# A two-layer graph network on one core: one-column bias products as steps of their own, the last norm in smaller steps, and a new order of all steps

## The chip, the core and the metric

The kernel runs on one core of one Trainium2 chip. The time is device microseconds of one execution, median of the runs shown. The engines are TensorE (PE, with its weight loads PEld), VectorE (DVE), ScalarE (ACT), GpSimd (POOL) and SyncE (SP), which here issues the DMAs.

## The reference

Input are 128 graphs of 128 nodes with 256 features, `x`, and their adjacency `adj` of 0 and 1, all in fp32. Two layers follow one another:

```
layer 0:  q, k = x@Wq+bq, x@Wk+bk          (8 heads of 32)
          attn = softmax(q k^T / sqrt(32))
          out  = sum over r of (attn * (adj == r)) @ (x@Wv[r]+bv[r])
          x    = LN(x + out@Wo+bo; g1, beta1)
          x    = LN(x + gelu(x@W1+b1)@W2+b2; g2, beta2)      (256 -> 1024 -> 256)
layer 1:  twice (W1,a1), (W2,a2):  Wh = h@W; e = leaky_relu(Wh1 + Wh2^T, 0.2)
          att = softmax over axis 1 of where(adj > 0, e, -9e15);  h = att@Wh
          x    = LN(x + h; g_ln1, b_ln1)
          x    = LN(x + relu(x@w_ff1+b_ff1)@w_ff2+b_ff2; g_ln2, b_ln2)
```

The kernel adds the second bias of a feed-forward part to the input of that part ahead of time, so the first bias has to be reduced by W1 applied to it: b1 - W1^T b2 in layer 0, b_ff1 - w_ff1^T b_ff2 in layer 1. These two corrections are the one-column products of this change.

## The kernel before

The 16384 nodes are worked on in 32 groups of 512 (four graphs each). What one group needs is cut into Python generators, and each `next` of one is a **step**: a few instructions, often one product or a piece of the chain behind it. `in_order` (L1141 on) walks through three strings, `FRONT`, `STEADY` and `TAIL`, and does one step for each token. A token `a:1*3` is three steps of generator `a` of the group one behind the base. `FRONT` runs once for groups 0 and 1 with all weight loads and set-up, `STEADY` runs for g = 1 to 29, `TAIL` runs from g = 30 to the end. All of it stands in a manual schedule, so the order of the tokens is the order of every engine's queue: PE, ACT, DVE, POOL, and SP with its DMAs. There is no other planner.

The tokens that are spoken of here:

- `in`, `rest`, `L...`: loads of xT, of adj and x, and of weights. All go through SP's queue.
- `q`: projections to q, k and v (pq, pv at L715 and L728; from group 2 on as Winograd forms pqqa, pqqb, pvqa, pvqb at L785). `a`: scores ps (L855), exp (ACT, L862), mask pm (DVE, L871), pav (L925), denominators pden (L913), the output product pwo (L965). `d`: sums over heads for the denominators, with a DMA (es<-e) on SP.
- `n0` to `n3`: layer norm: bn_stats (L407), variance + eps and power (L425 DVE, L426 POOL), two passes for each graph (L441 DVE: first with mean and gain, then with root and offset), then planes of 16 bits (L461 ACT) and a DMA transpose (L464). `t`: what comes back is copied (L489 ACT) and summed for the Winograd forms (yS, L498 to L502, DVE).
- `f`, `fc` and `k`, `kc`: the two feed-forward parts, their products (ph and seeded, L521; po and seeded, L530) and the chains behind them (activation hT, L545 ACT; sums at L588 to L663, mostly DVE). The products have few PSUM banks, so each waits for the chain that empties its bank.
- `l`: the attention of layer 1: pw (L1042), edges (L1013 ACT, gs at L1023 and L1031 DVE), py (L1055), pg (L1068).
- `b1`, `c1`: the bias corrections by `without` (L338), two steps each: sixteen one-column products into one PSUM tile `pbias`, then one subtraction of 128x8 on DVE. For b1 the column `temp` is a slice cut from the loaded b2; such slices share a buffer with the first hT tile of group 0.
- `w1`, `w2`, `u1`, `u2`, `wqk`, `wv`: sums of weight blocks (L262 DVE) for the Winograd forms. `output_bias`: the correction of bo (pb, L1117).
- `z`: the last norm of the last group. `out`: a store of a group's result. `checks`: minima and maxima for the flag.

PSUM tiles from `mm_tile` turn in two buffers of one tag ("s"). The same two serve ps, pqqa and pvqa alternately, pw, py, pg, pwo, pden of the second half, and pbias.

At the end, the last group's norm is done in two pairs of graphs. After `TAIL` the program compares the collected `c_out` with itself (`same`, `good`), does the passes of pair 0 and stores it, and then makes a flag from `good` with a product `pflag`; the flag decides whether a general version has to run over again.

Of the kernel before, what the change touches and what calls it, by code (L numbers as in the profile page):

```python
# [25 lines left out]
P = 128  # L26
G = 4
# [96 lines left out]
in:0 Lqk*2 q:0 Lqk L1 Lqk q:0*2 Lh1 Lgat Lv q:0 L2 Lv q:0 L4 Lv Lv_ Lg1 q:0*2 rest:0 Lv q:0 a:0  # L124
L1 Lv_ a:0*2 d:0 a:0*3 Lv_ d:0 q:0*2 L2 d:0*2 Lgat a:0 L1 Lg2 d:0*2 L1 in:1 d:0 a:0 q:0 d:0 a:0
q:0 a:0*6 wqk a:0*3 L2 a:0 L2 a:0 q:0*2 q:1 d:0*2 L1 d:0 a:0 rest:0 gw rest:1 d:0 a:0 L1 q:1 Lgat
w2 d:0*2 L3 Lo d:0 Lg1 q:1 a:0 d:0 q:0 L3 q:0 a:0 bo:0 q:1*3 w1 q:1 Lg1 q:1 L4 a:0 w2 a:0 a:1 w2
a:1*2 a:0*2 a:1 a:0 a:1 d:1 L3 bo:0 a:0 a:1*2 Lg1 a:0*2 d:1 a:0*2 rest:2 q:1 d:1 a:0 d:1 a:0 n0:0
q:1 n0:0 q:1 n0:0*2 q:1 b1 d:1*2 n0:0 a:1 d:1 w1 output_bias d:1 Lgat n0:0 a:1 Lh1 n0:0 t0:0*2 w1
bo:0 q:1 a:1 b1 a:1 L3 output_bias q:1 t0:0 a:1 f:0 a:1*3 w1 w2 a:1 d:1*2 a:1 t0:0 gw a:1 t0:0  # L130
Lh2 t0:0 d:1 fc:0 a:1 q:1 Lh1 a:1*2 f:0 fc:0 d:1 fc:0 a:1 f:0 d:1*3 f:0 fc:0 rest:1 f:0 q:1 a:1
f:0 gw d:1 a:1*2 f:0 fc:0*2 a:1*3 Lh1 f:0 fc:0*2 bo:1 L4 fc:0 wqk f:0 u1 fc:0 f:0 fc:0 a:1 in:2
fc:0 a:1 f:0 wqk a:1 fc:0 a:1 fc:0 f:0 fc:0 bo:1 a:1 L3 f:0 gw f:0*3 fc:0 a:1*2 q:2 fc:0*3 a:1
f:0 n0:1 L3 fc:0*4 L4 n0:1 f:0 fc:0 q:2 n0:1*2 fc:0 bo:1 f:0 n0:1 f:0 fc:0 Lg2 f:0 fc:0*2 q:2*2
t0:1 f:0 n0:1 fc:0 f:0 n0:1 f:0 q:2 fc:0 f:1 u2 fc:0*2 q:2 fc:1 t0:1 n1:0*2 gw n1:0*2 t0:1 q:2
t0:1 n1:0 q:2 t0:1*2 c1 n1:0 fc:1 n1:0 q:2 wv t1:0*2 q:2 u1 f:1 gelu t1:0 l:0 fc:1 t1:0 u1 u2
l:0*3 c1 q:2 wv f:1 q:2 l:0*2 wqk l:0 f:1 l:0 q:2 l:0 f:1 fc:1*2 f:1 fc:1 q:2 fc:1 f:1 q:2 f:1
fc:1*2 u2 exp q:2 f:1 l:0 wv fc:1*2 l:0*3 q:2*2 l:0*2 a:2 f:1 q:2 l:0 a:2 l:0 a:2 l:0*2 a:2*2
fc:1 l:0*6 f:1 a:2 l:0 wv l:0*2 d:2 fc:1*2 l:0 f:1 fc:1 u2 a:2 fc:1 f:1 fc:1 f:1 q:2 u1 fc:1 f:1
fc:1 f:1 l:0 fc:1 f:1 l:0*2 q:2*2 fc:1 d:2 f:1 l:0 fc:1 l:0 q:2 l:0 q:2 f:1 l:0 q:2 d:2 l:0 d:2  # L140
l:0*3 Lh2 d:2 a:2 l:0*2 fc:1 l:0*3 fc:1 l:0 fc:1 n2:0 q:2 n2:0*2 q:2 n2:0 q:2 fc:1 f:1 n2:0 fc:1
d:2 f:1 q:2
"""
STEADY = """
fc:0 q:1 d:1 q:1 fc:0 f:0 d:1 n2:-1*2 t2:-1*2 q:1 f:0 a:1 fc:0 a:1 f:0 fc:0 t2:-1 a:1*2 t2:-1
k:-1 t2:-1 a:1 fc:0 a:1 kc:-1 t2:-1 d:1 a:1 k:-1 a:1 k:-1 a:1 kc:-1 d:1 rest:1 n1:0 kc:-1 a:1
n1:0 d:1*2 a:1*2 k:-1*2 a:1 k:-1 a:1 k:-1 kc:-1 d:1 kc:-1 d:1 a:1 d:1 k:-1 in:2 d:1 k:-1*2 n1:0
a:1 kc:-1*2 a:1 n1:0*2 kc:-1*2 a:1 bo:1 kc:-1 a:1 kc:-1 a:1 k:-1 kc:-1 a:1*2 n1:0*2 a:1 kc:-1
t1:0*2 a:1 kc:-1 t1:0 a:1 k:-1 l:0 kc:-1 bo:1 a:1 l:0*2 kc:-1 t1:0 kc:-1 a:1 l:0 a:1 n0:1 k:-1*3
l:0*2 q:2 n0:1 l:0 kc:-1 q:2 k:-1 l:0 kc:-1 bo:1 k:-1 l:0 n0:1 kc:-1 k:-1 kc:-1*3 q:2*2 n0:1*3  # L150
kc:-1*2 n0:1 l:0*3 k:-1 t0:1 k:-1 t0:1 k:-1 kc:-1 k:-1 kc:-1*3 k:-1 kc:-1 l:0 k:-1 t0:1 f:1 t0:1
l:0 kc:-1 q:2 t0:1 fc:1 l:0 t0:1 f:1 l:0*2 f:1*3 l:0*2 fc:1*2 q:2 l:0 f:1 kc:-1 q:2 l:0 q:2 f:1
l:0*3 fc:1 l:0 rest:2 f:1 l:0 fc:1 l:0 n3:-1 f:1 l:0*2 fc:1*3 f:1 fc:1 n3:-1 fc:1 n3:-1 fc:1*2
q:2 f:1 fc:1 q:2*2 fc:1 q:2 f:1*2 fc:1 f:1 fc:1 q:2 f:1 fc:1 q:2 f:1 fc:1 gelu q:2*2 fc:1 q:2
l:0*3 fc:1 f:1 l:0 q:2 a:2 l:0 f:1 fc:1 l:0 fc:1 a:2 l:0 q:2 l:0*2 a:2 l:0 exp l:0 a:2*2 q:2 l:0
a:2 f:1 q:2 d:2 a:2 l:0 q:2 l:0*2 fc:1 d:2 q:2 l:0 d:2 fc:1 d:2 q:2*2 d:2 a:2 l:0 fc:1 n2:0 q:2
n2:0*2 q:2 out:-1 n2:0 q:2 fc:1 f:1 n2:0 q:2 d:2 f:1 fc:1
"""
TAIL = """
n2:-1 fc:0 d:1 n2:-1 q:1 fc:0 q:1 f:0 q:1 d:1 t2:-1 a:1 fc:0 t2:-1*2 f:0 a:1 f:0 fc:0 a:1 fc:0  # L160
n1:0 t2:-1 rest:1 t2:-1 n1:0 a:1*4 d:1 a:1 n1:0 k:-1 a:1 t2:-1 kc:-1 n1:0*2 k:-1 kc:-1 k:-1 bo:1
k:-1 d:1*3 n1:0 a:1 kc:-1 n1:0 k:-1 d:1 t1:0*2 k:-1 d:1 k:-1 a:1 kc:-1 d:1 kc:-1 k:-1 a:1*2 bo:1
k:-1 d:1 kc:-1 k:-1 kc:-1*2 a:1 t1:0 l:0*2 a:1 l:0 a:1*3 l:0 t1:0 bo:1 kc:-1*4 l:0 k:-1*2 a:1 l:0
a:1*2 l:0 kc:-1 l:0*2 kc:-1 a:1*3 kc:-1*2 a:1*2 k:-1*2 kc:-1 a:1 k:-1 a:1 n0:1 kc:-1 k:-1 kc:-1*4
l:0 n0:1 k:-1 l:0 k:-1 kc:-1 l:0*2 n0:1*2 k:-1 l:0*2 kc:-1*2 k:-1 n0:1*2 kc:-1 l:0 n0:1 l:0*2
k:-1 t0:1 l:0 kc:-1 l:0 kc:-1 t0:1 k:-1 l:0*2 t0:1 l:0 kc:-1 l:0 kc:-1 t0:1 l:0 t0:1 l:0*2 kc:-1
l:0 f:1 l:0 fc:1 t0:1 l:0*3 fc:1 k:-1 f:1 l:0 fc:1 f:1*2 l:0 fc:1 l:0*3 f:1*2 l:0 fc:1*2 l:0*2
f:1 fc:1*2 f:1 kc:-1 fc:1 f:1 l:0 fc:1*3 f:1*2 k:-1 fc:1 f:1 l:0 fc:1 f:1 fc:1 n3:-1 fc:1*2 f:1*2
fc:1 l:0 f:1 fc:1 l:0 fc:1 l:0*2 f:1 fc:1 n2:0 f:1 fc:1 n2:0 fc:1 n2:0 fc:1 n2:0 gelu f:1*2
fc:1*2 n2:0*2 n3:-1 n2:0 fc:1*2 t2:0 fc:1 t2:0 f:1*3 exp t2:0 f:1 fc:1*3 k:0 t2:0 n1:1 t2:0 kc:0  # L170
n1:1*2 k:0 n1:1 k:0 n1:1*2 t2:0 k:0 n1:1 k:0 kc:0 k:0 kc:0 t1:1*3 k:0 kc:0 l:1*3 t1:1 l:1 kc:0*2
l:1*3 k:0 kc:0 l:1*2 k:0 kc:0*3 l:1*2 kc:0 l:1*3 kc:0 l:1 k:0 l:1 k:0 l:1 kc:0 k:0 l:1*2 kc:0 k:0
kc:0 l:1*2 n3:-1 l:1*7 kc:0*2 l:1*4 k:0 l:1*2 k:0 l:1*3 kc:0 l:1 kc:0 k:0*2 l:1*2 kc:0 l:1 kc:0*2
l:1 kc:0 l:1*4 kc:0 n2:1 kc:0 k:0 n2:1*4 k:0 kc:0 k:0 n2:1 kc:0 n2:1 t2:1 kc:0 k:0 t2:1 k:0 kc:0
t2:1 kc:0*2 k:0 k:1 t2:1*3 kc:1 k:1 k:0 kc:1*2 k:1*2 kc:1 k:1 kc:0 kc:1 k:1 kc:1 k:1 kc:1 k:1
kc:1*2 out:-1 kc:1 k:1*2 kc:1*2 k:1 kc:1 k:1 n3:0 kc:1 n3:0 k:1*3 kc:1*2 k:1*2 checks kc:1*6 k:1
kc:1 k:1 kc:1*2 n3:0 k:1*2 kc:1 k:1 kc:1*4 k:1 out:0 k:1 z:1 kc:1*2 z:1*2
# [11 lines left out]
def fast_pass(ctx, tc, a, out):  # L189
# [148 lines left out]
    def without(b, w, col):  # L338

        pb = mm_tile("pbias")  # L340
        for f in range(NF):
            h, m = divmod(f, NF // 2)
            for c in range(NCH):
                nc.tensor.matmul(
                    pb[:, f : f + 1], w[:, PLAIN[c][h], 0, m * P : (m + 1) * P],
                    col[:, c : c + 1], start=(c == 0), stop=(c == NCH - 1),
                )
        yield
        nc.vector.tensor_sub(b, b, pb[:, :NF])
        yield 1  # L350
# [61 lines left out]
    def added(S, i, p, po):  # L412
# [1114 lines left out]
```

## Time and profile before

| | us |
|---|---|
| median of 3 runs | 2650.34 (2647.93 to 2650.73) |
| the profiled execution | 2649.95 |
| its span, first to last instruction | 2648.2 |
| mean granted clock of TensorE | 0.994 |

Four stretches of 40 us of the first 160, one of the steady part and two of the tail, as busy microseconds of each engine:

| us | PE | PEld | DVE | ACT | granted clock |
|---|---|---|---|---|---|
| 0 to 40 | 35.08 | 20.11 | 16.88 | 16.43 | 0.96 |
| 40 to 80 | 34.13 | 28.42 | 29.34 | 21.82 | 0.90 |
| 80 to 120 | 40.00 | 35.86 | 32.05 | 19.47 | 0.88 |
| 120 to 160 | 34.93 | 28.90 | 22.71 | 27.13 | 0.91 |
| 2560 to 2600 | 35.64 | 29.90 | 29.72 | 27.44 | 1.00 |
| 2600 to 2640 | 36.37 | 33.22 | 31.36 | 15.16 | 1.00 |

PE's records overlap: a record of a product lasts longer than the time after which the next one starts. So a busy share near 100% doesn't say that PE ran at its peak, and the starts of successive products tell more than their lengths. In the timeline the columns are start, length, engine, line, operation, output and inputs by name, shapes and count, and in brackets an idle time before it with what released it. One product of the program shows as two records (fp32), so a product of two instructions of 256 columns is "x4". The groups of the steady part follow one another about every 80 us; the second pg product of a group starts at 235.0 in the first of them, and the following ones on average 80.4 us apart up to 2405.9.

### The profile page before, as it was taken

The page shows a single profiled execution, that of the slowest core. Times are in us where ns is not written, and L with a number is a line of the kernel's source. Part 1 is how long each engine was busy: PE and PEld are TensorE (multiplying, and loading weights), DVE is VectorE, ACT ScalarE, POOL GpSimd, SP SyncE. Part 2 cuts the span into 40 slices and gives each one's busy share as a digit, 9 for nine tenths or more (in the row PEclk, how much of TensorE's full clock was granted, in tenths as well). Part 3 has the DMA queues.
Part 4 walks back from the last instruction along what each step waited for, and adds up shares of the span by engine and source line. Part 5 has one row for each costly group of instructions (what it writes and reads, how often), then busy time and mean ns, then how long its engine had stood idle before and what let it go on. Part 6 is the DMA issues. An engine that isn't in the chain of part 4 may idle for free.

```text
span 2648.2 us, 54505 instructions
## 1 busy us (share of the span) xinstructions
PE 2603.5 (98%) x20842; PEld 2309.2 (87%) x20842; DVE 2246.1 (85%) x5907; ACT 1859.7 (70%) x3839; POOL 132.8 (5%) x137
## 2 busy tenths in 40 slices
PE   9999999999999999999999999999999999999998
PEld 6788988889888889888889888889888898888887
DVE  5688888888888888888888888888888888898876
ACT  4567676777776776776776776777767767767764
POOL 0000000000000000000000000000000000000000
PEclk9899999999999999999999999999999999999999
DMA  6223223322223322223232323222233223232311
GB/s 179 57 55 73 49 64 65 74 61 55 61 58 73 74 64 48 66 61 73 61 71 51 67 62 73 61 66 53 55 73 73 64 45 69 61 73 61 69 29 34
DMA packets 317372, 170.61 MB, mean 64 GB/s; under 512 B 222768, under 2 KB 295600, under 8 KB 317104
## 3 DMA queue, kind: packets, MB, share of 16 engines
q1 hardware_dynamic: 316000, 166.66, 28.0%
q8 instruction: 166, 2.72, 0.4%
q14 instruction: 102, 0.84, 0.1%
q10 hardware_dynamic: 1104, 0.40, 0.1%
HBM read 66.20 MB, written 16.90 MB: 31 GB/s over the span
## 4 chain that ended last, share of the span: by engine, by line
PE 74%; DVE 14%; ACT 8%; issue 2%; DMA 2%; SPq 0%; POOL 0%; DVEq 0%; ACTq 0%; POOLq 0%
PE po L530 15%; PE ph L521 12%; PE seeded L521 10%; PE seeded L530 9%; PE pw L1042 4%; PE pwo L965 4%; PE pqqa L785 4%; PE pqqb L785 3%; PE pav L925 3%; DVE x L441 2%; ACT pm L896 2%; PE py L1055 2%; DVE st L407 2%; PE pvqa L785 2%; ACT e L862 2%
## 5 line engine op out<-in xcount | busy, mean ns | idle before, releaser
L461 ACT COPY planes<-x 128x512 uint16<-128x512 uint16 x384 | 223.5, 615 | 197.8 <-DVE x L441 197.0
L489 ACT COPY yT<-pT 128x512 uint16<-128x512 uint16 x384 | 272.0, 764 | 114.0 <-DMA pT<-planes 113.7
L426 POOL TENSOR_TENSOR rs<-rs,mhalf 128x4 f32<-128x4 f32 x129 | 130.7, 1013 | 2444.2 <-DVE rs L425 1749.2
L862 ACT ACTIVATE e<-ps 128x512 f32<-128x512 f32 x256 | 136.2, 589 | 98.4 <-PE ps L855 65.0
L521 PE MATMUL ph<-yT,w_L_gnn_w_ff 128*128 128x256 f32 x768 | 198.3, 387 | 6.5 <-ACT hT L545 6.2
L521 PE MATMUL seeded<-yS,w_L_gnn_w_ff 128*128 128x256 f32 x768 | 199.9, 383 | 2.9 <-DVE yS L501 1.8
L521 PE MATMUL seeded<-yS,w_L_gnn_W 128*128 128x256 f32 x768 | 201.9, 386 | 0.0
L521 PE MATMUL ph<-yT,w_L_gnn_W 128*128 128x256 f32 x768 | 197.3, 379 | 0.0
L407 DVE BATCH_NORM_STATS2 st<-x 128x6 f32<-128x256 f32 x512 | 191.2, 415 | 3.5
L530 PE MATMUL po<-w_L_gnn_W,hT 128*128 128x128 f32 x1536 | 187.1, 275 | 0.0
L530 PE MATMUL po<-w_L_gnn_w_ff,hT 128*128 128x128 f32 x1536 | 187.0, 275 | 0.0
L530 PEld LDWEIGHTS po<-w_L_gnn_W,hT 128*128 128x128 f32 x1536 | 184.0, 192 | 3.2
L530 PEld LDWEIGHTS po<-w_L_gnn_w_ff,hT 128*128 128x128 f32 x1536 | 181.7, 192 | 1.7
L871 DVE TENSOR_TENSOR pm<-e,adj 128x512 f32<-128x512 f32 x256 | 172.2, 683 | 2.9 <-ACT e L862 0.7
L521 PEld LDWEIGHTS ph<-yT,w_L_gnn_w_ff 128*128 128x128 f32 x768 | 140.6, 190 | 38.9 <-ACT hT L545 18.5
L521 PEld LDWEIGHTS seeded<-yS,w_L_gnn_w_ff 128*128 128x128 f32 x768 | 141.8, 190 | 31.0 <-ACT seeded L617 6.4
L521 PEld LDWEIGHTS seeded<-yS,w_L_gnn_W 128*128 128x128 f32 x768 | 143.3, 191 | 28.0 <-ACT seeded L644 6.2
L521 PEld LDWEIGHTS ph<-yT,w_L_gnn_W 128*128 128x128 f32 x768 | 143.5, 190 | 18.4
L896 ACT COPY pm<-e 64x512 f32<-64x512 f32 x256 | 157.8, 616 | 1.6
L545 ACT ACTIVATE hT<-hT,c_L_gnn_b 128x256 f32<-128x256 f32 x256 | 112.7, 500 | 48.9 <-DVE hT L629 29.7
L545 ACT ACTIVATE hT<-hT,c_L_gnn_b_ff 128x256 f32<-128x256 f32 x256 | 115.7, 501 | 26.1 <-DVE hT L629 22.9
L1042 PE MATMUL pw<-wu,yT 128*128 128x260 f32 x512 | 130.6, 387 | 2.7 <-ACT yT L489 2.6
(195 smaller groups left out, 6288.1 us busy)
## 6 DMA issues: line engine op xcount, KB each, us to landing
es<-e SPq DMA_DIRECT2D x256, 128.0 KB, 2.4
xT<-in_xT_dram SPq DMA_DIRECT2D x32, 512.0 KB, 4.9
x<-in_x_dram SPq DMA_DIRECT2D x32, 512.0 KB, 4.2
out_dram<-x SPq DMA_DIRECT2D x31, 512.0 KB, 3.3
spread<-hbm SPq DMA_DIRECT2D x61, 256.0 KB, 3.9
adj<-in_adjT_dram SPq DMA_DIRECT2D x32, 256.0 KB, 3.1
pT<-planes SPq DMA_TRANSPOSE x192, 3.1
w_L_gnn_W<-in_L_gnn_W_dram SPq DMA_DIRECT2D x8, 256.0 KB, 4.8
```

What stands on the lines that cost most here:

```text
L407: nc.vector.bn_stats(st[:, b % 2, :], S["x"][:, b, :])
L426: nc.gpsimd.tensor_tensor(rs[:, bs], rs[:, bs], k.mhalf[:, bs], op=ALU.pow)
L461: nc.scalar.copy(planes[:, :, b], words)
L489: nc.scalar.copy(o.rearrange("p (b t h) -> p h b t", b=2, h=2), pT[:, :, :, c, :])
L521: nc.tensor.matmul(bank[:, s * TH : (s + 1) * TH], wa[:, form, 0, f * P : (f + 1) * P], m, start=start and s == 0, stop=True, skip_group_c ...
L530: nc.tensor.matmul(bank[:, s * P : (s + 1) * P], m[:, f, s * P : (s + 1) * P], wb_[:, form, f, :], start=start and s + f == 0, stop=True, ...
L545: nc.scalar.activation(o[:, s], o[:, s] if src is None else src[:, s * TH : (s + 1) * TH], func, bias=ba[:, f : f + 1],)
L785: nc.tensor.matmul(bank[:, s * TH : (s + 1) * TH], *ops, start=start and s == 0, stop=True, skip_group_check=True,)
L862: nc.scalar.activation(e[:, s], pss[s], AF.Exp, scale=SCALE)
L871: nc.vector.tensor_mul(pm[:, s], S["e", p][:, s], S["ad"][:, pair(p), None, :].to_broadcast([P, 2, NCH, P]),)
L896: nc.scalar.copy(ea[own], e[own, hs, lo].rearrange("p s c i -> p s (c i)"))
L1042: nc.tensor.matmul(pw[:, :NU], yT[:, c, b * P : (b + 1) * P], wu[:, c, :], start=(c == 0), stop=(c == NCH - 1),)
```

## The change

Three things are changed together.

1. `without` yields eight times instead of twice. Each step has two one-column products (four records) for one block of 128 outputs into a tile of its own, and its own one-column subtraction. The number of products is as before; the subtractions are sixteen of 128x1 instead of two of 128x8. The new strings put these steps among larger products.
2. In the last norm, the two passes of pair 1 are two steps, the second with the store. `root` of pair 0 no longer notes its result in `c_out`; after `TAIL` the passes and the store of pair 0 come first, then the note, then `same` and `good`.
3. All three strings are new. The steps and their inner order are the same except for 1 and 2, but how the generators are interleaved differs throughout, and with it the queues of all engines, the DMAs included.

```diff
 FRONT = """
-in:0 Lqk*2 q:0 Lqk L1 Lqk q:0*2 Lh1 Lgat Lv q:0 L2 Lv q:0 L4 Lv Lv_ Lg1 q:0*2 rest:0 Lv q:0 a:0
+Lqk*2 in:0 q:0*2 L1 q:0 Lqk Lv Lqk wqk q:0*4 Lv q:0 a:0 Lv a:0*2 Lv L2 L1 a:0*2 rest:0 L1 Lv_ a:0
...
-t0:1 f:0 n0:1 fc:0 f:0 n0:1 f:0 q:2 fc:0 f:1 u2 fc:0*2 q:2 fc:1 t0:1 n1:0*2 gw n1:0*2 t0:1 q:2
-t0:1 n1:0 q:2 t0:1*2 c1 n1:0 fc:1 n1:0 q:2 wv t1:0*2 q:2 u1 f:1 gelu t1:0 l:0 fc:1 t1:0 u1 u2
+gw q:2*2 c1 q:2 t0:1 n1:0 c1 n1:0 f:1 q:2*2 n1:0 t0:1 q:2 t0:1 fc:1 n1:0 c1 n1:0 q:2*2 f:1 t1:0
...
 STEADY = """
-fc:0 q:1 d:1 q:1 fc:0 f:0 d:1 n2:-1*2 t2:-1*2 q:1 f:0 a:1 fc:0 a:1 f:0 fc:0 t2:-1 a:1*2 t2:-1
+f:0*2 a:1 f:0 q:1*3 n2:-1*2 t2:-1 fc:0 a:1 t2:-1*2 a:1*2 t2:-1 f:0 fc:0 k:-1 t2:-1 a:1 t2:-1 fc:0
...
 TAIL = """
...
-kc:1*2 out:-1 kc:1 k:1*2 kc:1*2 k:1 kc:1 k:1 n3:0 kc:1 n3:0 k:1*3 kc:1*2 k:1*2 checks kc:1*6 k:1
-kc:1 k:1 kc:1*2 n3:0 k:1*2 kc:1 k:1 kc:1*4 k:1 out:0 k:1 z:1 kc:1*2 z:1*2
+kc:1*3 k:1 kc:1*2 n3:0 kc:1*2 k:1*2 n3:0 kc:1*2 k:1*2 kc:1*3 out:-1 k:1*2 out:0 z:1 kc:1*2 z:1
+kc:1 z:1*2
...
     def without(b, w, col):
 
-        pb = mm_tile("pbias")
         for f in range(NF):
             h, m = divmod(f, NF // 2)
+            pb = mm_tile("pbias")
             for c in range(NCH):
                 nc.tensor.matmul(
-                    pb[:, f : f + 1], w[:, PLAIN[c][h], 0, m * P : (m + 1) * P],
+                    pb[:, :1], w[:, PLAIN[c][h], 0, m * P : (m + 1) * P],
                     col[:, c : c + 1], start=(c == 0), stop=(c == NCH - 1),
                 )
-        yield
-        nc.vector.tensor_sub(b, b, pb[:, :NF])
-        yield 1
+            nc.vector.tensor_sub(b[:, f : f + 1], b[:, f : f + 1], pb[:, :1])
+            yield 1
...
+    def noted(S, bs):
+        nc.vector.scalar_tensor_tensor(
+            c_out[:, bs], S["mv", 3][:, bs], 0.0, c_out[:, bs], op0=ALU.mult, op1=ALU.add
+        )
...
-    def affine(S, i, bs=slice(0, G)):
+    def affine(S, i, bs=slice(0, G), passes=(True, False)):
...
-        for first in (True, False):
+        for first in passes:
...
         def last_norm(S):
             root(S, 3, pair(1))
             yield 1
-            affine(S, 3, pair(1))
+            affine(S, 3, pair(1), (True,))
+            yield 1
+            affine(S, 3, pair(1), (False,))
             store(S, pair(1))
             yield 1
-            root(S, 3, pair(0))
+            root(S, 3, pair(0), now=False)
             yield 1
...
         S1 = st[NG - 1]
+        affine(S1, 3, pair(0))
+        store(S1, pair(0))
+        noted(S1, pair(0))
         same = flat(w1p.tile([P, G, P], F32, tag="gs", name="same"))[:, : G * 2]
...
-        affine(S1, 3, pair(0))
-        store(S1, pair(0))
```

In the new order of PE's queue, the places that differ and that the prediction speaks of are these. All four pv products of group 0 stand ahead of its first pav; pq of group 1 and ps of group 1 follow before the second pav. Between the products of the first feed-forward part of group 0, the correction b1 is dealt out as eight steps from just behind the first pv of group 1 to among the first ph and seeded products of group 0; c1 follows among pqqa, pqqb and ph of groups 2 and 1, with four of its steps shortly before ps of group 2 and the last before po of group 1. In the steady group the two pg products stand side by side, and the four edge steps on ACT (L1013) that they rest on come well before them; in the second feed-forward part three products instead of two stand between a ph product and the next one into the same bank; the pw products come behind both pwo; the py products are dealt one at a time among others. On SP the load of xT of group 0 comes third instead of first, behind two weight loads, and the load of layer 1's b_ff2 comes before the es transfers of group 1's second half.

## The prediction, made before the change was run

> **What bounds the kernel now.** I read the page from the top: the engine totals, then the chain of work that ended last.
>
> ```profile
> PE 2603.5 (98%) x20842; PEld 2309.2 (87%) x20842; DVE 2246.1 (85%) x5907; ACT 1859.7 (70%) x3839; POOL 132.8 (5%) x137
> ...
> PE 74%; DVE 14%; ACT 8%; issue 2%; DMA 2%; SPq 0%; POOL 0%; DVEq 0%; ACTq 0%; POOLq 0%
> ```
>
> TensorE sets the time, and DVE is the engine that it most often waits for. The change takes no product away: the columns that pass through PE stay the same. All it can save is time in which PE waits or runs slowly, and busy PE of 98% hides that, because a product that waits inside its run, or that runs at half clock, still counts as busy. So I read the PE rows of the timeline by their starts. An undisturbed product of four records of 128x256 takes 0.86 us from start to start (1378.98 to 1379.85 below), a head block of pav and pden 2.31 us (1374.60 to 1376.91). Every longer step is loss. Adding these losses up gives 109 us before the last product ends: 36 in the first 160 us, about 60 in the steady groups (1.9 to 2.3 per group), 17 after 2480.
>
> Steady state, the windows of 40 us and then PE's timeline in one group:
>
> ```profile
> 1360.00:1400.00 40.00, 39.78 (x370) 34.59 (x369) 39.04 (x100) 26.20 (x53) 3.02 (x3) 1.00 0.37 87
> ```
> ```profile
> 1374.60 0.42 PE L925 MATMUL pav<-e,v 128*32 128x128 f32 x8
> ...
> 1376.91 1.17 PE L855 MATMUL ps<-qT,kT 32*128 32x128 f32 x32
> ...
> 1378.98 1.03 PE L521 MATMUL ph<-yS,w_L_gnn_w_ff 128*128 128x256 f32 x4
> 1379.85 1.09 PE L521 MATMUL seeded<-yS,w_L_gnn_w_ff 128*128 128x256 f32 x4
> ...
> 1382.50 1.03 PE L521 MATMUL seeded<-yS,w_L_gnn_w_ff 128*128 128x256 f32 x4
> 1383.75 1.13 PE L521 MATMUL ph<-yT,w_L_gnn_w_ff 128*128 128x256 f32 x4 [0.22 <-ACT hT L545]
> ...
> 1437.72 1.03 PE L785 MATMUL pvqa<-w_v,xT 128*128 128x256 f32 x4
> 1438.76 1.10 PE L1068 MATMUL pg<-yh,gs 128*128 128x256 f32 x4
> ```
>
> The step from 1382.50 to 1383.75 is 1.25 us, 0.38 over the usual; that from 1437.72 to 1438.76 is 1.04, 0.18 over. DVE is busy 39.04 of 40 us here: it runs just behind PE, and whatever is put ahead of a DVE result that PE needs is felt.
>
> The front, PE's timeline and then windows cut at these places (columns: window, length, busy time of PE, PEld, DVE, ACT and POOL, granted clock, DMA share, GB/s):
>
> ```profile
> 51.70 3.73 PE L344 MATMUL pbias<-temp,w_L_gnn_W 128*128 128x1 f32 x32
> 55.30 2.05 PE L1117 MATMUL pb<-w_L_gnn_Wo,temp 128*128 128x256 f32 x4
> 57.15 2.56 PE L728 MATMUL pv<-w_v,xT 128*128 128x256 f32 x8
> ...
> 75.91 0.64 PE L925 MATMUL pav<-pm,v 128*32 128x128 f32 x2 [4.38 <-DVE pm L871]
> ...
> 114.50 2.05 PE L521 MATMUL seeded<-yS,w_L_gnn_W 128*128 128x256 f32 x4
> 116.35 1.91 PE L785 MATMUL pqqa<-xS,w_qk 128*128 128x256 f32 x4
> ...
> 134.49 2.09 PE L855 MATMUL ps<-qT,kT 32*128 32x128 f32 x32 [3.01 <-ACT kT L805]
> ```
> ```profile
> 55.30:59.60 4.30, 4.30 (x13) 3.30 (x13) 4.26 (x10) 3.10 (x6) 0.00 (x0) 0.63 0.78 186
> ...
> 114.50:121.70 7.20, 7.20 (x22) 5.89 (x23) 2.48 (x6) 4.06 (x9) 0.00 (x0) 0.62 0.19 36
> 121.70:126.00 4.30, 4.30 (x22) 3.76 (x21) 0.17 (x1) 3.17 (x8) 0.00 (x0) 1.00 0.03 4
> ```
>
> **The bias products.** Each run of 32 records takes 3.60 us (51.70 to 55.30), 0.11 a record, and stays: sixteen steps of four records are 16 x 0.45 = 7.2 us either way. What goes is what follows a run. After the first, pb and pv take 1.85 and 2.49 us where 0.86 and 1.73 are usual (1.75 lost). Around the second, the run itself takes 4.16 instead of 3.60, and the next three products 5.26 instead of 2.59 (3.25 lost with the pw behind them). The clock column says why: 0.63 and 0.62, then 1.00. [...] PE is busy in every microsecond of the runs[...]; by the rows, one-column products don't count as work for the clock, and 5.0 us go once a run is 0.45 us long. I take the rows. [...]
>
> Each step also takes a buffer of its own and gives it back only when its one-column subtraction has passed DVE's queue. The 128x8 one takes 0.16 us, so fourteen more cost DVE 2.2 us. No row shows this wait. Below: -0.09 a step, if loads hide under neighbours (the 128x2 products at 109.03 step at 0.09 instead of 0.11 a record, 0.4 us in all at that rate, 1.4 at most). Above: 1 us a step, since the old subtraction came 4 us after its run, behind 4 us of DVE work, and two to three products of 0.86 lie between two takings. I take 0.1, 1.6 us. Net -3.4.
>
> **The front's order.** The start puts two weight loads ahead of xT on SP; the loads are issued about 0.5 us apart, so xT comes 1 us later[...]: nothing. The first pav block takes 6.55 us (20.94 to 27.49) against 2.31; now all four pv products stand ahead of it, two of them new there, 2 x 1.72 of cover. pq of group 1 and the next ps come earlier and meet ACT's exp sooner, about 1.3 us given back with the wait at ps: net -3. The block at 70.90 takes 10.37 us against 2.31, 8.1 lost. It waits for a DVE product queued behind work that could not start before hT had its buffer, which the slice of L1's b_ff2 held until its load (issued at 67.6, landed at 72.3). The new order issues that load ahead of group 1's es transfers; I count three new waits of about 1.2 us in its place (DVE's yS and v, then the second pav): -4.5. At 134.49 PE waits 3.2 us for kT and then runs at half clock (7.80 us to 142.29 where 4.57 are usual, 3.2 more). Four bias steps and a product now stand there, 2.7 us of cover: -4.4 with 2 us kept for new waits. pg at 155.17 waits 2.0 us for gs; its L1013 chain is now earlier: -1. With the bias steps' 3.4 that is -16.3; other places in a front as dense as this will miss their inputs, +2.3 assumed. **Front: -14.**
>
> **The steady order.** Per group I can name: the wait at pg 0.26 (0.18 and the next), at ph for hT 0.38, at the pw products for yT 0.23 (1392.41 to 1393.46 is 1.05, the rest behind it), and smaller ones of 0.06 to 0.14 each, together 0.57. About 0.1 at each change of shape remains. In the new order the two pg products stand together with their ACT chain well before, three products instead of two stand between hT's source and its user, and the pw products come after pwo: these three go, -0.87, and half of the small ones, -0.28. New: a product closer behind DVE's L629 sum (0.15) and pav closer behind its last mask L871 (0.2), and 0.1 for what I can't place: +0.45. That is -0.7 a group, times 28.5: **-20.** Where cover is lost, DVE is next.
>
> **The tail.** Named PE waits after 2480 sum to 6.3 us without the flag's, the largest at yS (1.78, 1.28) and gs (1.22). The new tail moves the gs chain and yS forward; I take half, -3. At the very end all DVE work stays; the last store starts after 1.7 us of passes instead of after flag work as well, 0.9 us earlier, while the flag reaches PE some 0.5 us later. The span ends 5.6 us behind the flag and 3.5 behind the store's landing; between -0.9 and +0.5, I take 0. **Tail: -3.**
>
> **Sum.** 2648.2 - 14 - 20 - 3 = 2611.2 of span; the 1.75 us around it make 2613.0. The profiled run stands 0.4 below the median of 2650.34, so 2613.
>
> **The rivals.** *Waits move on* (0.24): each wait removed uncovers the next, DVE at 39 of 40 being the limit. Steady -0.3 x 28.5 = -9, front -8, tail -1: 2632. For it: DVE's share; against: from 1400.40 to 1432.85 hardly a PE step is over its usual length, so DVE isn't late everywhere. *More goes than I count* (0.12): steady -1.3, nearly all of the 1.44 I can name, -37; front -20, tail -5: 2588. *Slower* (0.05): one DVE-fed product of the steady order, most likely pav behind L871 or ph behind L629, stands too early and waits in every group. From (20 + 14 + 3) / 28.5 = 1.3 us a group it eats the gain; at 1.7 the time is 2661. Against it: in my count the DVE queue has 0.2 to 0.6 us to spare before pav. *The change does next to nothing* (0.03): an order with the same losses elsewhere, 2650. The forecast itself has 0.56, with its own range 2601 to 2624.
>
> Range for 8 in 10: down to 2592, which takes in half of the larger gain (0.06), and up to 2638, which takes in three quarters of the moved waits (0.18): 0.56 + 0.06 + 0.18 = 0.80. A change within 0.2% (5.3 us) can't be told from none here. Faster 0.92, same 0.03, slower 0.05.
>
> **What would show it.** Bias steps right: granted clock near 1.00 from 50 to 126 us, none of the 128x256 products at 1.7 us. Front right: first pg of group 1 (233.2 now) near 219. Steady right: pg to pg of the next group near 79.7 us instead of 80.4, with no 0.22 wait of ph for hT; wrong if pav or ph now waits for DVE in most groups. Tail right: the waits at yS and gs below 3 us together. The forecast fails if the steady period is 80.2 or more.

## The result and the profile after

The changed kernel takes 2632.55 us (median of 6 runs, 2631.74 to 2633.71), the kernel before 2648.09 in the same runs: a ratio of 0.9942, with the interval 0.9929 to 0.9955. That is 15.5 us, faster as forecast and inside the range, but well under half of the 37 us that were forecast. 2632 is the time that was written beside the rival "waits move on".

First the page of the kernel after: span, engine totals, the row of granted clocks and the chain.

```profile
span 2631.9 us, 54467 instructions
...
PE 2598.8 (99%) x20842; PEld 2302.5 (87%) x20842; DVE 2246.7 (85%) x5921; ACT 1857.4 (71%) x3839; POOL 141.8 (5%) x137
...
PEclk9999999999999999999999999999999999999999
...
PE 92%; DVE 3%; DMA 2%; ACT 2%; issue 1%; SPq 0%; POOL 0%; ACTq 0%; POOLq 0%; DVEq 0%
```

Busy PE fell by only 4.7 us, so most of the gain is time in which PE stood still or ran slowly. Before, the row of granted clocks had an 8 in its second place, which has gone. The windows of the front (length, then busy PE, PEld, DVE, ACT, POOL, granted clock, DMA share, GB/s):

```profile
40.00:80.00 40.00, 36.74 (x396) 30.52 (x393) 34.12 (x96) 24.53 (x48) 2.62 (x3) 1.00 0.68 171
80.00:120.00 40.00, 39.79 (x258) 36.90 (x257) 31.05 (x85) 26.59 (x58) 2.37 (x2) 1.00 0.18 34
120.00:160.00 40.00, 36.88 (x335) 31.76 (x334) 34.34 (x97) 25.23 (x49) 2.02 (x2) 1.00 0.23 60
```

Clocks of 0.90, 0.88 and 0.91 have become 1.00. Over the three windows together DVE is busy 99.5 us where it was 84.1, and ACT 76.4 where it was 68.4: the front's work has moved forward.

To find where the time went, the starts of PE's products were compared with the usual steps, as in the prediction, in both traces. The start of the first pg of a group serves as a milestone. A step is irregular here when it is longer than the length at which most steps stand.

| stretch | before | after | difference |
|---|---|---|---|
| span's start to the first pg of group 1 | 233.19 | 218.14 | -15.05 |
| mean from pg to pg, 26 steady steps | 80.40 | 80.28 | -0.12, so -3.4 for 28 |
| the same, at the length of the undisturbed steps | 80.00 | 80.13 | +0.13 |
| start of the last steady group's pg to the last large product | 151.05 | 153.25 | +2.2 |
| last large product's start to the span's end | 13.09 | 13.03 | 0 |

So in the traces the front gave nearly the whole gain, and the steady order, from which 20 us were expected, 3.4. (The steady steps end at 2484.06 before and at 2465.63 after.)

### The profile page after: what moved, and what is told of

Its sections match the earlier page's. It is cut to its first block, busy times and chain, and to the rows that moved or that the text cites. A ratio compares the mean times of both kernels' runs of the same rounds, so it can differ in the third digit from the quotient of the medians.

```text
span 2631.9 us, 54467 instructions
## 1 busy us (share of the span) xinstructions
PE 2598.8 (99%) x20842; PEld 2302.5 (87%) x20842; DVE 2246.7 (85%) x5921; ACT 1857.4 (71%) x3839; POOL 141.8 (5%) x137
## 4 chain that ended last, share of the span: by engine, by line
PE 92%; DVE 3%; DMA 2%; ACT 2%; issue 1%; SPq 0%; POOL 0%; ACTq 0%; POOLq 0%; DVEq 0%
PE po L534 16%; PE ph L525 16%; PE seeded L525 13%; PE seeded L534 12%; PE pwo L969 4%; PE pav L929 4%; PE pw L1046 4%; PE pqqa L789 4%; PE pvqa L789 4%; PE pqqb L789 3%; PE pvqb L789 3%; PE ps L859 2%; PE py L1059 2%; PE pg L1072 2%; PE pden L917 1%; DVE x L445 1%
## 5 line engine op out<-in xcount | busy, mean ns | idle before, releaser
L431 POOL TENSOR_TENSOR rs<-rs,mhalf 128x4 f32<-128x4 f32 x129 | 139.5, 1081 | 2430.7 <-DVE rs L430 1836.9
L525 PE MATMUL seeded<-yS,w_L_gnn_w_ff 128*128 128x256 f32 x768 | 208.8, 394 | 2.8 <-ACT seeded L621 1.6
L525 PEld LDWEIGHTS seeded<-yS,w_L_gnn_w_ff 128*128 128x128 f32 x768 | 135.7, 189 | 51.3 <-ACT p L629 16.1
L633 DVE TENSOR_TENSOR hT<-seeded,p 128x512 f32<-128x512 f32 x128 | 87.6, 684 | 90.6 <-PE seeded L525 87.1
L900 ACT COPY pm<-e 64x512 f32<-64x512 f32 x256 | 157.6, 616 | 2.3
L629 ACT COPY p<-seeded 128x512 f32<-128x512 f32 x128 | 75.0, 586 | 97.0 <-PE seeded L525 96.7
```

What stands on the lines that cost most here:

```text
L431: nc.gpsimd.tensor_tensor(rs[:, bs], rs[:, bs], k.mhalf[:, bs], op=ALU.pow)
L525: nc.tensor.matmul(bank[:, s * TH : (s + 1) * TH], wa[:, form, 0, f * P : (f + 1) * P], m, start=start and s == 0, stop=True, skip_group_c ...
L900: nc.scalar.copy(ea[own], e[own, hs, lo].rearrange("p s c i -> p s (c i)"))
```

## The experiments

All times are medians beside runs of the kernel before on the same chip; the kernel before stood at 2646.9 to 2648.6 there. "Below" and "above" are counted from the changed kernel's 2632.55 us unless before is named. Two runs of different chips are compared with some 2 us of doubt for that reason.

| run | us | ratio to before, interval |
|---|---|---|
| front_only | 2632.91 | 0.9939 (0.9923 to 0.9956) |
| steady_only | 2649.84 | 1.0004 (0.9995 to 1.0013) |
| tail_old | 2632.01 | 0.9943 (0.9926 to 0.9960) |
| norm_only | 2648.36 | 1.0005 (0.9996 to 1.0015) |
| bias_bundled | 2649.15 | 1.0003 (0.9994 to 1.0012) |
| bias_one_tile | 2645.77 | 0.9992 (0.9984 to 1.0001) |
| b1_run | 2639.57 | 0.9971 (0.9960 to 0.9982) |
| deal_only | 2654.12 | 1.0023 (1.0015 to 1.0032) |
| none_new | 2628.93 | 0.9923 (0.9906 to 0.9941) |
| none_old | 2647.74 | 1.0002 (0.9993 to 1.0010) |
| spaced | 2678.72 | 1.0112 (1.0095 to 1.0129) |
| spaced_two | 2642.01 | 0.9979 (0.9970 to 0.9987) |
| dve_less | 2633.49 | 0.9945 (0.9929 to 0.9962) |
| dve_more | 2636.36 | 0.9956 (0.9939 to 0.9973) |
| act_more | 2641.11 | 0.9972 (0.9962 to 0.9982) |
| act_less | 2633.82 | 0.9943 (0.9926 to 0.9959) |

### One part of the change at a time

**front_only**: the new FRONT, all else of before.

```diff
-        for g in range(1, NG - 2):
+        in_order(FIRST, 1)          # the old STEADY, fitted to the new front's end
+        for g in range(2, NG - 2):
             in_order(STEADY, g)     # the old STEADY, then the old TAIL
```

> The new FRONT with the dealt bias steps; STEADY, TAIL and the last norm as before (at the seam the first STEADY is adjusted by the few steps in which the two fronts differ). Theory 'the front carries it' (read from the two traces: 15 us of PE losses gone before the first steady group, 3 in the steady groups, 2 given back in the tail): 15 us below before, 2631 to 2635. Rival 'as forecast' (front -14, steady -20, tail -3, something else lost): also -14 here, so the two are told apart by the steady run. Rival 'the steady order carries it': less than 5 below before.

2632.9: the front carries all of it that the times can show.

**steady_only**: the kernel before with the new STEADY, fitted at both seams in the same way.

> The new STEADY alone, FRONT, TAIL, bias runs and last norm as before. Theory 'spacing' (the new order removes the waits at pg, ph and pw, but alternates ph and seeded so that the seeded bank is used again after one product): 2 to 5 us below before, pg to pg 80.1 in most groups. Rival, the forecast: 20 below before, pg to pg 79.7. Rival 'worse alone': not below before.

2649.8, no difference from before. Its trace has the new period (80.13 in most steps, 80.29 on average), which is 3.0 us less for 28 steps; but its first steady group starts 1.6 us later, and the old tail behind it is longer by 2.4 us. That is less than the 2 to 5 us expected by the first theory, and far from the forecast's 20.

**tail_old** and **norm_only**: the changed kernel with the TAIL of before; and the kernel before with the new last norm.

```diff
-k:1*2 kc:1 k:1 kc:1*4 k:1 out:0 k:1 z:1 kc:1*2 z:1*2
+k:1*2 kc:1 k:1 kc:1*4 k:1 out:0 k:1 z:1 kc:1 z:1 kc:1 z:1*2      (norm_only)
```

> The changed kernel with the TAIL of before (adjusted at the seam); the order at the very end, passes and store of pair 0 ahead of the flag, stays new. Theory from the traces (the new tail is 2 us longer than the old, most of it one wait of 3.4 us for yS and the half rate behind it): 1.5 to 3 us below the changed kernel. Rival: the tail waits move on, within 1 us.

> The kernel before with the change to the last norm alone (first pass of pair 1 between the last sum and its statistics, passes and store of pair 0 ahead of the flag). The forecast: between 0.9 below and 0.5 above, none that can be measured. Rival: the earlier store ends the program 1 us sooner, with the landing of the last store nearer the last product. Rival: the later flag costs 0.5.

With the old tail the profiled span is 2.1 us shorter, but only 1.0 of that lies behind the start of the last steady group, and the medians stand 0.5 apart, within their spread: not settled by the times. The last norm changes nothing that can be measured. The new tail's longest wait, in PE's timeline of the changed kernel:

```profile
2556.03 2.02 PE L525 MATMUL ph<-yS,w_L_gnn_w_ff 128*128 128x256 f32 x4 [3.45 <-DVE yS L502]
```

The wait for yS in group 31, 1.28 us before, is 3.45 now, and the product behind it takes 2.02 us (1.03 is usual): the granted clock is 0.50 from 2556.06 to 2559.48 us. The order that was to move yS forward brought it later. (The old tail has a wait of 1.78 us for yS elsewhere that the new one has not.)

### The bias products

**bias_bundled**: all eight steps of each correction at the place of the first.

```diff
-q:1 a:0 b1 d:1 a:0 a:1 L2 bo:0 q:1 d:1
-a:0*2 n0:0 q:1 b1 L2 n0:0 b1 output_bias ...
+q:1 a:0 b1*8 d:1 a:0 a:1 L2 bo:0 q:1 d:1
+a:0*2 n0:0 q:1 L2 n0:0 output_bias ...
```

> The changed kernel, but the eight b1 steps stand together where the first of them was, and the eight c1 steps likewise; each step keeps its own tile and subtraction. Theory 'one-column products do not count as work for the clock': the granted clock falls to about 0.6 behind each bundle, 4 to 6 us above the changed kernel. [...] Rival 'tiles': two buffers and sixteen subtractions behind DVE's queue make the bundles wait for each other, over 8 us, with waits of pbias for DVE in the trace.

2649.2: the whole gain is gone, more than any of the theories gave. In PE's timeline the steps of the second bundle wait for each other's subtraction, and the product behind them takes 2.05 us where 1.03 is usual; the granted clock from 80 to 120 us is 0.87:

```profile
109.70 5.28 PE L345 MATMUL pbias<-c_L_gnn_b_ff,w_L_gnn_w_ff 128*128 128x1 f32 x24 [1.24 <-DVE c_L_gnn_b_ff L349]
114.84 2.05 PE L789 MATMUL pqqa<-xT,w_qk 128*128 128x256 f32 x4
```

The two bundles took 5.5 us longer than two runs of 3.6 us (the 24 records shown step over 5.14 us, where 0.11 a record makes 2.7); the products behind them lost another 5.5 us (the three behind the second bundle take 2.05, 1.91 and 1.67 us where 1.03 is usual); the rest of the 16.6 came as later waits. To part these, **bias_one_tile** went back to one tile and one subtraction, in the new order:

```diff
     def without(b, w, col):
+        pb = mm_tile("pbias")
         for f in range(NF):
             ...
-            nc.vector.tensor_sub(b[:, f : f + 1], b[:, f : f + 1], pb[:, :1])
-            yield 1
+        yield
+        nc.vector.tensor_sub(b, b, pb[:, :NF])
+        yield 1
```

> The changed kernel with the bias corrections as they were: sixteen one-column products in a row into one tile, one subtraction, at the places of the first dealt step and of the fourth. The order of all other steps stays new. In the run with bundled steps the whole gain was gone (0 against before, 16.6 above the changed kernel); its trace shows 5.5 us of half-rate products behind the bundles, 5.6 us in which the steps of a bundle waited for each other's tiles, and later waits. Theory 'clock plus knock-on': with one tile the 5.6 go, the half rate stays: 5 to 11 us above the changed kernel. Rival 'it was all the tiles': within 2 us of the changed kernel, clock near 1.00. Rival 'the row of sixteen, however stored': 14 us or more above.

2645.8, 13 us above. The separate tiles were only some 3 of the 16.6 us. PE's timeline around the second run, and the windows cut there:

```profile
105.14 4.43 PE L345 MATMUL pbias<-c_L_gnn_b_ff,w_L_gnn_w_ff 128*128 128x1 f32 x32
109.44 2.05 PE L790 MATMUL pqqa<-xT,w_qk 128*128 128x256 f32 x4
111.28 1.91 PE L526 MATMUL ph<-yT,w_L_gnn_W 128*128 128x256 f32 x4
112.99 1.90 PE L790 MATMUL pqqb<-xT,w_qk 128*128 128x256 f32 x4
114.69 1.06 PE L790 MATMUL pqqa<-xS,w_qk 128*128 128x256 f32 x4
```
```profile
109.40:114.70 5.30, 5.30 (x14) 4.22 (x15) 0.32 (x1) 2.31 (x5) 0.00 (x0) 0.50 0.11 21
114.70:118.00 3.30, 3.30 (x17) 2.91 (x16) 2.05 (x4) 2.36 (x6) 0.00 (x0) 0.99 0.41 79
```

Nothing waits here (PE is busy in all of the 4.30 us from 105.10): the run goes on for 4.3 us, the next three products step by 1.84, 1.71 and 1.70 us instead of 0.86, at a granted clock of 0.50, and then the clock is back at 0.99. So half clock came behind this row of one-column products though PE was busy all the time. And the two runs cost 13 us, more than the 7 us of half clock that follow them in this trace.

It need not come, though. In before half clock stands behind both runs (0.50 from 55.08 to 58.50 and from 113.11 to 119.94 us), in bias_one_tile behind both as well (3.6 and 3.4 us lost). Behind the second run of norm_only, whose FRONT is that of before, token by token, it doesn't. PE's timeline there:

```profile
110.59 3.63 PE L344 MATMUL pbias<-c_L_gnn_b_ff,w_L_gnn_w_ff 128*128 128x1 f32 x32
114.08 1.11 PE L525 MATMUL seeded<-yS,w_L_gnn_W 128*128 128x256 f32 x4
115.03 1.03 PE L789 MATMUL pqqa<-xS,w_qk 128*128 128x256 f32 x4
```

The next step is 0.95 us and the one behind it 0.86, and from 100 to 120 us this trace loses 0.15 us where before loses 3.5. The windows around the second run, for pbias alone (busy time of PE, PEld and DVE, then the clock), in before and in norm_only:

```profile
109.70:113.11 3.41, 2.77 (x26) 2.96 (x26) 0.00 (x0) 1.00 0.28 54
113.11:119.94 6.83, 1.53 (x8) 1.44 (x7) 0.16 (x1) 0.50 0.26 50
```
```profile
108.78:112.19 3.41, 1.59 (x16) 1.78 (x16) 0.00 (x0) 1.00 0.00 0
112.19:115.60 3.41, 2.03 (x19) 1.95 (x18) 0.00 (x0) 1.00 0.66 128
115.60:119.01 3.41, 0.00 (x0) 0.00 (x0) 0.15 (x1) 1.00 0.14 25
```

In before the clock was 0.50 for 6.83 us from 113.11 on; in norm_only it stood at 1.00 from 108.78 to 119.01 us. Why the same row brought half clock in one and not in the other is not shown.

**b1_run** made only the first correction a run:

```diff
+    def without_run(b, w, col):      # the old function, two steps
...
-            b1=without(b1, w1, b2c), c1=without(c1, u1, c2c),
+            b1=without_run(b1, w1, b2c), c1=without(c1, u1, c2c),
```

> The changed kernel with b1 as one run into one tile (at the places of its first and fourth step) and c1 still dealt. With both as runs it was 13 us above the changed kernel; the trace there shows half clock behind each run, 3.6 and 3.4 us, and later waits behind each. Theory 'each run brings its own': 5 to 8 us above the changed kernel. Rival 'it is the first run, whose delay goes on through the front': 11 us or more. Rival 'it is the second': 2 or less.

7 us above: the first run brings about half of the 13.

**deal_only** took the kernel before and put one bias step behind each of the next products, nothing else.

```diff
-n0:0 q:1 n0:0*2 q:1 b1 d:1*2 n0:0 a:1 d:1 w1 output_bias d:1 ...
+n0:0 q:1 n0:0*2 q:1 b1 d:1*2 n0:0 a:1 d:1 w1 output_bias b1 d:1 ...
```

> The kernel before with only the bias corrections dealt out, one step behind each of the next products, all strings otherwise as before. Theory 'the half rate is a cost of its own': 4 to 6 us below before, the granted clock at 1.00 from 50 to 126 us, while the holes at 71 and 134 us stay. Rival 'dealing only pays with the new front': within 1.5 us of before. Rival 'tiles cost': slower than before.

2654.1: slower than before. Its waits in PE's timeline:

```profile
53.76 1.13 PE L1116 MATMUL pb<-w_L_gnn_Wo,temp 128*128 128x256 f32 x4 [1.94 <-DVE c_L_gnn_b L348]
...
69.62 1.33 PE L520 MATMUL ph<-yS,w_L_gnn_W 128*128 128x256 f32 x4 [2.90 <-DVE yS L497]
...
115.18 2.07 PE L520 MATMUL seeded<-yS,w_L_gnn_W 128*128 128x256 f32 x4 [2.46 <-DVE yS L500]
...
139.59 0.81 PE L854 MATMUL ps<-qT,kT 32*128 32x128 f32 x8 [3.02 <-ACT kT L804]
```

The first line is the price of a tile of its own: pb waits 1.94 us for the one-column subtraction, which stands in DVE's queue. The hole at 139.59 is the one that stood at 134.49 before (3.01 us), 5 us later, untouched. And half clock came here too: the product behind the wait of 2.46 us takes 2.07 us where 1.03 is usual, and the window 80 to 120 has a granted clock of 0.93. So dealing didn't even save that.

Then both orders without any bias products, every b1 and c1 taken out of FRONT (the biases that they fold in are zero in these data):

```diff
-q:1 n0:0*2 q:1 b1 d:1*2 n0:0 a:1
+q:1 n0:0*2 q:1 d:1*2 n0:0 a:1
...
```

> The kernel before with the two bias runs left out. By the forecast's rows the runs cost 7.2 us and 5.0 of half clock, 12 us below before, and the new order alone would be worth none_old minus none_new, some 10 us. Rival 'the order alone is worth the whole': 7 us below before, the holes at 71 and 134 us as they were. Rival 'the old order without runs is as good as the new': 20 us or more below before.

> The changed kernel with the sixteen bias steps left out of FRONT (the second biases are zero, so the output is the same). Theory 'dealt well, a step costs its weight loads': 16 x 0.45 = 7.2 us and some 2 of waits, so 7 to 9 us below the changed kernel. Rival 'the steps fill holes that PE has anyway': 4 us or less below. Rival 'the steps disturb more than they take': over 11 below.

These two show how the gain splits. Taking the 7.2 us of one-column products out of the **old** order gains nothing (2647.7 against 2646.9). Taking the dealt steps out of the **new** order gains 3.6 us, or 2.4 when each is set against the kernel before of its own runs. PE's waits in the old order without them:

```profile
56.99 0.41 PE L924 MATMUL pav<-pm,v 128*32 128x128 f32 x2 [1.91 <-DVE pm L870]
59.01 0.39 PE L924 MATMUL pav<-pm,v 128*32 128x128 f32 x1 [1.62 <-DVE pm L870]
76.68 0.63 PE L924 MATMUL pav<-pm,v 128*32 128x128 f32 x2 [4.58 <-DVE pm L870]
...
113.85 2.05 PE L520 MATMUL seeded<-yS,w_L_gnn_W 128*128 128x256 f32 x4 [2.89 <-ACT planes L460]
...
132.53 1.17 PE L854 MATMUL ps<-qT,kT 32*128 32x128 f32 x32 [3.01 <-ACT kT L804]
```

PE only follows here. The wait of 4.58 at 76.68 stands at nearly the moment of the old 4.38 at 75.91, though the products ahead of it are fewer: its mask comes when DVE's queue brings it. In front of it 3.5 us of new waits have taken the place of the first run, and 2.89 us at 113.85 that of the second. Nor did half clock go with the runs: behind the wait of 2.89 us the product takes 2.05 us where 1.03 is usual, and the three windows have a granted clock of 0.90, 0.93 and 0.96. So in these stretches the old front is bound by what feeds PE; the new order, by itself, is worth 2647.7 - 2628.9 = 19 us. In the new order PE is closer behind its inputs, and there the products do cost time: 2 to 4 us for sixteen dealt steps, 15 to 17 for two runs (2645.8 - 2628.9, or each against its own before).

### The steady group

Each half of a feed-forward part has three products into the seeded bank of PSUM (called T2, T1 and B22, in this order); T4 is the last of its ph products. After steady_only the question was why the named waits had gone and the group hadn't become shorter. One stretch of a steady group of the changed kernel, all engines, from the timeline (the second feed-forward part of layer 1, first half):

```profile
401.56 0.59 ACT L629 COPY p<-seeded 128x512 f32<-128x512 f32 x1 [0.27 <-PE seeded L525]
...
402.20 0.73 PEld L525 LDWEIGHTS seeded<-yS,w_L_gnn_w_ff 128*128 128x128 f32 x4 [0.27 <-ACT p L629]
402.20 1.13 PE L525 MATMUL seeded<-yS,w_L_gnn_w_ff 128*128 128x256 f32 x4
...
402.95 0.84 PEld L525 LDWEIGHTS ph<-yT,w_L_gnn_w_ff 128*128 128x128 f32 x4
403.17 1.03 PE L525 MATMUL ph<-yT,w_L_gnn_w_ff 128*128 128x256 f32 x4
403.44 0.69 DVE L633 TENSOR_TENSOR hT<-seeded,p 128x512 f32<-128x512 f32 x1
...
404.18 0.73 PEld L525 LDWEIGHTS seeded<-yS,w_L_gnn_w_ff 128*128 128x128 f32 x4 [0.39 <-DVE hT L633]
404.19 1.13 PE L525 MATMUL seeded<-yS,w_L_gnn_w_ff 128*128 128x256 f32 x4
...
404.94 0.84 PEld L525 LDWEIGHTS ph<-yT,w_L_gnn_w_ff 128*128 128x128 f32 x4
405.15 1.03 PE L525 MATMUL ph<-yT,w_L_gnn_w_ff 128*128 128x256 f32 x4
```

Follow the seeded bank. Its product starts at 402.20 and its last record ends at 403.33. DVE takes it up at 403.44 and has done at 404.13, and the next seeded product starts at 404.19. Between lies one ph product of 0.86 us, from 403.17 to 404.03: too short by 0.16. There is a second price. The waiting product's weight load starts with it (404.18 and 404.19), while that of an undisturbed product leads by 0.22 (402.95 and 403.17); so its step is 0.97 instead of 0.86, 0.105 more. Here a wait of 0.16 costs 0.26, and the product at 402.20, which comes only 0.03 later than an undisturbed one would, steps by 0.97 as well. Before, two products stood between these uses of the bank, and the wait was at ph (0.38 + 0.105, the steps from 1382.50 and 1383.75 in the prediction's lines).

**dve_less** and **dve_more** test the other explanation, that DVE paces the group. The first leaves out two small reductions for the flag in groups 2 to 29, the second does them twice. They stand in the attention part, not in the stretch shown.

```diff
-        nc.vector.tensor_reduce(c_att[:, 0, g, p : p + 1], each, AX.X, ALU.min)
-        nc.vector.tensor_reduce(c_att[:, 1, g, p : p + 1], each, AX.X, ALU.add)
+        if g < 2 or g >= NG - 2:            # dve_more: both once more if 2 <= g < NG - 2
+            nc.vector.tensor_reduce(c_att[:, 0, g, p : p + 1], each, AX.X, ALU.min)
+            nc.vector.tensor_reduce(c_att[:, 1, g, p : p + 1], each, AX.X, ALU.add)
```

> The changed kernel without the two small DVE reductions of each half of the attention denominators (smallest and sum, which feed the flag alone) in groups 2 to 29; their table is set to 1 at the start. 4 x 0.17 = 0.7 us of DVE work less in each group, PE's and ACT's work and all orders as before. Theory 'DVE paces the stretch where PE waits' (three reorderings moved the waits and shortened nothing): 0.2 to 0.7 us a group, 6 to 20 us below the changed kernel. Rival 'spacing' (the waits are the length of each chain from a product's end through one DVE or ACT instruction to the next product): within 3 us of the changed kernel, pg to pg 80.1 in most groups.

> The changed kernel with the same two reductions done twice in groups 2 to 29: 0.7 us of DVE work more in each group. Theory 'DVE paces': 0.4 us a group or more, 10 to 20 us above the changed kernel. Rival 'spacing': within 5 us of it.

2633.5 and 2636.4; in both most steps from pg to pg are 80.13 us, as in the changed kernel. The same stretch in the timeline of dve_more:

```profile
402.74 1.13 PE L525 MATMUL seeded<-yS,w_L_gnn_w_ff 128*128 128x256 f32 x4
403.71 1.03 PE L525 MATMUL ph<-yT,w_L_gnn_w_ff 128*128 128x256 f32 x4
404.72 1.13 PE L525 MATMUL seeded<-yS,w_L_gnn_w_ff 128*128 128x256 f32 x4
```

Steps of 0.97 and 1.01 us (0.97 and 1.02 in the changed kernel), with 0.7 us more on DVE. So the load of DVE doesn't set these waits; what is left is the length of the chain from a product's end through one DVE or ACT instruction to the next use of the bank. A shorter instruction in that chain was not tried. (Of the 3.8 us of dve_more, 2.2 stand in irregular steps.)

**act_more** and **act_less** do the same for ACT: one copy of planes twice, and the same copy on GpSimd.

```diff
             nc.scalar.copy(planes[:, :, b], words)
+            if i == 1 and p == 0 and b == 0 and 2 <= S["g"] < NG - 2:   # act_less: on gpsimd instead
+                nc.scalar.copy(planes[:, :, b], words)
```

> The changed kernel with one copy on ACT (planes of the second norm, first half) done twice in groups 2 to 29: 0.6 us of ACT work more in each group, in the stretch where PE alternates ph and seeded. Theory 'DVE paces': within 4 us of the changed kernel. Theory 'ACT paces': 8 to 17 us above. Rival 'spacing': within 4 us.

> The changed kernel with one copy a group (planes of the second norm, first half) moved from ACT to GpSimd in groups 2 to 29: 0.6 us of ACT work less where PE alternates ph and seeded. Theory 'spacing': within 3 us of the changed kernel, pg to pg 80.13 in most groups. Rival 'ACT paces': 6 to 17 us below. Rival 'the copy is slower on GpSimd or disturbs DVE, and its transpose comes late': above the changed kernel, with waits of pw for yT.

More ACT work costs 8.6 us: most steps are 80.38, and all of the 0.25 is in one place, behind the first pwo, where seeded waits for ACT's copy. Less gains nothing: 80.13. ACT has little room at that place, but taking that copy from it doesn't shorten the group.

If spacing is the cause, more spacing should help. **spaced** moved T4 ahead of T1, so that two products stand between uses of the seeded bank, in three of the four half feed-forward parts, and masks and an activation forward to match; **spaced_two** only in the second halves (its edit is shown; the larger one does the same to the first half of `k`).

```diff
-kc:-1 k:-1 a:1 t1:0 k:-1 kc:-1 t1:0 k:-1 t1:0 a:1 kc:-1*2 k:-1 l:0*2
+kc:-1 k:-1 a:1 t1:0 k:-1*3 kc:-1 t1:0*2 a:1 kc:-1*2 l:0*2
...
-f:1 fc:1 q:2 rest:2 f:1 fc:1*2 l:0 f:1 l:0 q:2 l:0 fc:1*2 l:0 q:2 f:1 q:2
+f:1 fc:1 q:2 rest:2 f:1*3 fc:1*2 l:0*2 q:2 l:0 fc:1 l:0 q:2*2 fc:1
```

> The changed kernel with STEADY alone reordered: in three of the four half feed-forward parts of a group the product T4 goes ahead of T1 and the last product of the half two or more places on, so that two products or more stand between uses of the seeded bank; masks on DVE and one activation on ACT go earlier to match. Theory 'spacing' (each use after one product costs 0.03 to 0.16 of wait and 0.105 because its weights are not loaded ahead): 0.4 to 0.8 us a group, 11 to 22 us below the changed kernel, pg to pg 79.3 to 79.7. Rival 'DVE is the limit of a group': within 3 us of the changed kernel, the waits back at pav or ph for DVE. Rival 'new waits': slower than the changed kernel.

> The changed kernel with STEADY reordered only in the second half of each feed-forward part: T4 ahead of T1, the last product of the first part's half two places on; masks and the first halves are left alone (the larger reordering put a mask ahead of a sum that still read its buffer, and made ACT wait 2 us a group). Theory 'spacing': the waits of 0.14 at each of the two places go, 0.27 a group: 6 to 9 us below the changed kernel, pg to pg 79.86 in most groups. Rival 'DVE or ACT is the limit of a group': within 2 us.

Both are slower than the changed kernel. In spaced, copies on ACT (L900) overwrote masks that were now made before them, so part of the attention used wrong masks; its instructions are the same, and its times show the waits of this order. In its timeline:

```profile
328.54 1.25 ACT L900 COPY pm<-e 64x512 f32<-64x512 f32 x2 [2.02 <-DVE pm L875]
...
334.80 1.13 PE L525 MATMUL seeded<-yS,w_L_gnn_w_ff 128*128 128x256 f32 x4 [0.89 <-ACT seeded L648]
```

ACT waits 2.02 us for DVE, is late with all that it has to do next, and seeded pays 0.89 (and a step 1.15 over the usual) for it. In spaced_two the waits at the two places did go, 0.14 each; in their place the group waits 0.27 ahead of the first po, and 0.25 at pg again: 80.40 in most steps. So the waits at a bank do go with the spacing, as spaced_two shows, but in both orders another result came late, and neither was shorter in all.

No run's median lies below the range of the changed kernel except that of none_new, which leaves work out.

## Why the prediction was partly wrong

**What held.** The front's sum: -14 forecast, -15 measured, the first pg of group 1 at 218.1 where 219 was written. The granted clock of 1.00 from 50 to 126 us: 1.00 in all three windows of the changed kernel. That half clock can stand behind one-column products in a row: shown by bias_one_tile (0.50 behind 4.3 us of them). But the 5.0 us were read from one trace as if they came every time; the second run's share of them was missing in norm_only. The hole at 71 us: forecast -4.5, and the losses from 60 to 80 us fell from 7.9 to 3.8. The one at 134: -4.4, and from 120 to 140 they fell from 6.1 to 2.4. The end and the last norm: 0 and 0.

**What failed: the steady order.** Forecast were -20 us and a period of 79.7; measured were -3.4 and 80.28, past the 80.2 that the prediction named as its sign of being wrong. The step is "these three go, -0.87, and half of the small ones, -0.28 ... New ... +0.45. That is -0.7 a group". In an undisturbed group the waits named at pg (0.26) and hT (0.49 with its late weight load) did go, with 0.07 of small ones: 0.82. The wait at the pw products went too: it stood in 10 of 28 groups before, 0.23 a group on average, and stands in none now. So what went is 1.05 a group, close to the 1.15 forecast. But in its place came 0.40 in the first half of the second feed-forward part (0.03, 0.105, 0.16 and 0.105), 0.16 at pav, 0.14 in the second half, and 0.24 in the first feed-forward part's second half: 0.94. So the new term was 0.94, not 0.45, and 0.94 - 1.05 is the -0.11 or -0.12 of the mean. Two of its parts were named, behind L629 and at pav. What was missed is that T2, T1 and B22 all go through one bank, with a single ph between them now, and that such a wait carries another 0.105 (a step of 0.97 instead of 0.86), its weight load not being ahead. dve_less, dve_more and act_less speak against the load of the engines as the cause; that the chain at the bank is the cause is read from the trace and from the two waits that went in spaced_two, and no order that kept the gain at pg, hT and pw without the new waits was found.

**The tail** was forecast at -3 and came out at +2 in the trace: the order of the tokens seemed to bring yS forward, and in group 31 the wait for it grew by 2.2 us, with a granted clock of 0.50 behind it. The times don't settle this term (tail_old).

**Right sum, wrong split.** That the front's sum came out right is in part luck. Its terms were treated as independent, and they aren't. Dealing was -3.4 in the sum: alone it is +6, in the new order -13. The new order alone was some -10: with the runs left in it is -2.8, without bias products -19. The tiles of the bias steps were taken at 0.1 us a step; in the old order they cost more (1.94 us at pb). The first pav, -3 in the sum, gave about 1 (the losses from 20 to 40 us fell from 5.4 to 4.6): pq's own wait of 1.69, which costs 1.8, took most of the rest.

**The rivals.** "Waits move on" had the time right, but by luck: it took 9 from the steady groups and 8 from the front, where 3 and 15 went. Waits did move on in the steady group, not in the front, and the runs speak against DVE's load as the reason.

## What to carry to other kernels

Before you subtract a wait, ask what else is late at that moment: here a bank that was used again after one product of 0.86 us, before it had been emptied, gave a new wait of 0.16 us, and the weight load that could not run ahead added 0.105. Take the work itself away once (none_old did): if nothing is gained, the stretch is bound elsewhere, and a cheaper form of that work is worth nothing there until the order is changed. Terms that touch the same queue and the same tiles aren't summed; they are measured together, and apart. And a half-clock stretch read from one trace is looked for in a second one before it is entered as a cost.

## What was not expected of the hardware

A product of four records that had waited stepped by 0.97 us instead of 0.86, its weight load starting with it instead of 0.22 us ahead: in the changed kernel at 402.20 and 404.19, in before at 1383.75 (the next one starts at 1384.72). The step of 0.97 stands in dve_more too (402.74 to 403.71).

Half clock came behind a row of one-column products (bias_one_tile: 0.50 in the window after 4.3 us of them), with waits of 2.9 to 3.0 us (in none_old 2.89, the product behind it 2.05 us instead of 1.03; in before 3.01 at 134.49, with 0.50 from 133.59 to 140.42 us), and in none_new behind three waits of 0.89, 0.88 and 0.73 us close together, with a clock of 0.72 from 65.4 to 71.6 us. In the changed kernel, with waits of 0.66, 0.95 and 0.34 us at the same place and bias steps between the products, the clock stayed at 1.00 (40 to 80 us). What decides between these cases is not shown: no run was made to test it.
